# Conv and attention kernel on one core: engines issue in the order of the text, chains end where their buffers are taken anew, positions are loaded two chunks ahead, three chunks are projected early

## The chip, the cores and the metric

The kernel runs on one core of one Trainium2 chip. The metric is the device time of one execution in microseconds (us). The kernel before takes 2003.53 us (median of 3 runs, 2001.35 to 2005.6).

Five engines matter: TensorE (PE in the profile; PEld is its weight load), VectorE (DVE), ScalarE (ACT), GpSimd (POOL) and SyncE (SP), which only issues transfers here. In the built program each engine has its own list of instructions, and an instruction that needs the result of another engine waits for it.

## The reference

Eight images of 128 channels and 48 x 48 = 2304 positions. Cut to what matters:

```python
# layer 0: group norm, projections with position channels, causal attention
xg = group_norm(x)                                   # 32 groups
x0 = concat([xg, pe])                                # 32 position channels
q, k, v = (leaky_relu(W @ x0 + b) for W, b in ...)   # 128 x 2304 each
x = x + softmax(causal(q.T @ k / sqrt(128))) @ v
# layer 1, on tokens
t = tokens(x)
y = layer_norm(t);  t = t + softmax(y @ y.T) @ y     # full attention
y = layer_norm(t);  t = t + recurrence(batch_norm(y @ W.T))   # a scan over 8 batches
```

Everything is float32.

## The kernel before

A batch has six chunks (`NQ`) of 384 columns (`QC`), three blocks of 128 (`QB`) each. A batch is a causal attention followed by a full attention; the eight batches follow one another, and the recurrence closes the kernel. In the full attention some exponentials are stored to DRAM turned (`e`) and loaded back (`g`), so that they are not computed twice. The attention loop is software pipelined: scores of item n are issued, then the product of item n - lag, then `st.tick` may issue one step of the side work (projections, norms, tails of finished chunks), which waits in *chains*:

```python
class Stream:
    def run(self, chain):
        work, cost, delay = chain.steps.popleft()
        work()
        self.now += cost
        chain.at = self.now + delay
        ...
    def tick(self, cost):
        self.now += cost
        for chain in self.chains:
            if chain.at <= self.now:
                self.run(chain)
                return
```

`now` is a clock of the text: it counts the estimated TensorE time of what has been written so far. A step comes into the text when this clock says that its inputs should be there. In the kernel before, the text is only a proposal: a scheduler in the build orders the instructions of each engine anew.

The parts of the causal attention that the argument touches:

```python
def begin(j, m, first):
    if first:
        st.finish(projected[b, j])
        if j + 2 < NQ:
            projected[b, j + 2] = st.add(project(b, j + 2))
    s = psum_s(...);  matmul(s, keys, queries[b, j])
    p = pp.tile(...);  nc.scalar.activation(p, s, Exp)
    if m >= QB * j:                                   # three diagonal blocks come first
        nc.gpsimd.tensor_mul(p[:, off:off+P], ..., triu)      # the mask, on GpSimd
    ...  nc.vector.tensor_add(acc, acc, p)            # row sums

def causal(j, o):                                     # after the last product of chunk j
    def residual():
        tp = psum_t(...);  matmul(tp, ones, acc)      # dn
        nc.vector.reciprocal(r, tp)
        nc.vector.tensor_mul(r, o, r)
        nc.gpsimd.tensor_add(t1, xt, r)               # the residual, on GpSimd too
    ...                                               # tokens (tt), normed (xhT), back (tb)
    st.add([(residual, 0.7, 5.5), (tokens, 0.5, 4.5), (normed, 0.0, 2.0), (back, 0.5, 0.0)])

attention(listed(chunks), 2, begin, product, causal)  # lag 2
```

In `project`, `normed` loads the positions `pb` of a chunk where they are used, then `xn` and three products `pj` follow, each with `z = pj + pb`, a leaky ReLU and a maximum on VectorE. In the full attention, `full` has a chain of six steps for each finished chunk: sums, residual (`ot`), keep (`tk`), normed (`x`), back (`tx`, `xc`), statistics (`wx`). Chunks 0 and 1 of the next batch are projected during the full attention.

## Time and profile before

| | kernel before |
|---|---|
| time, median of 3 | 2003.53 us |
| span of the profiled run | 2000.6 us, mean granted clock 0.978 |
| PE / DVE / ACT / POOL busy | 94 / 64 / 37 / 13% |
| one batch (from the chain of waits) | 227.0 us |

TensorE is the bound, so what counts is the time that it stands idle, or runs at half clock afterwards (four products of 384 columns from 715.79 us start 0.63 us apart instead of 0.32, and the granted clock from 713 to 721 us is 0.79). The prediction shows the lines for this. Two more views are needed later. First the waits of TensorE, largest first; the columns are what waited, for what, us in total, how often, and the longest:

```profile
PE o_causal L913 <- DVE r L926: 21.6, 9, 3.9
PE tx L846 <- DVE x L841: 19.1, 9, 2.2
```

The wait for a mask is far down the list: 0.9 us, once. Second, the timeline of GpSimd at the start of a causal chunk (start, busy us, what, and in brackets the idle time before it and its releaser):

```profile
571.20 0.45 POOL L897 TENSOR_TENSOR p<-p,triu 128x128 f32<-128x128 f32 x1 [7.29 <-ACT p L895]
572.17 0.46 POOL L897 TENSOR_TENSOR p<-p,triu 128x128 f32<-128x128 f32 x1 [0.52 <-ACT p L895]
573.57 0.46 POOL L897 TENSOR_TENSOR p<-p,triu 128x128 f32<-128x128 f32 x1 [0.95 <-ACT p L895]
576.30 1.18 POOL L928 TENSOR_TENSOR t<-x,r 128x384 f32<-128x384 f32 x1 [2.27 <-DVE r L926]
```

The scheduler has put the three masks of the new chunk first (so it is in every chunk of the built program), each running as soon as its exponential is done, and the residual of the finished chunk (`t<-x,r`), which waits for VectorE, behind them.

### The profile page before, as it was taken

The numbers are of one execution on the slowest core, as the hardware profiler recorded it, in microseconds if no ns is written. First come the engines' busy times: TensorE is split into PE (matmuls) and PEld (weight loads), VectorE is DVE, ScalarE is ACT, GpSimd is POOL, SyncE is SP. The second block draws the span as 40 slices with busy tenths as digits, with TensorE's granted clock in tenths as the row PEclk, the third lists the DMA queues.
The fourth block names the chain that finished last, engine by engine and source line by source line (L and its number), as shares of the span: only waits on it lengthen the run. The fifth ranks groups of instructions, "written<-read, shape, count | busy, mean of one in ns | idle before, by whom it ended". The sixth has DMA issues, their size and how long they took to land.

```text
span 2000.6 us, 22146 instructions
## 1 busy us (share of the span) xinstructions
PE 1884.1 (94%) x6760; PEld 1153.8 (58%) x6760; DVE 1280.1 (64%) x3174; ACT 740.6 (37%) x1940; POOL 258.0 (13%) x359
## 2 busy tenths in 40 slices
PE   7899989999999989999999999999999999999793
PEld 4556656665566656665566655665566655665462
DVE  5577558764877558764777559765677549663263
ACT  2244323442245313442245423442245413442352
POOL 1110012001110112001110112101110112101000
PEclk9999999999999999999999999999999999999897
DMA  2105530354105530344205531344205530244504
GB/s 85 42 29 183 150 95 24 107 177 113 66 12 193 154 103 24 107 160 116 80 12 182 159 98 36 107 150 115 91 12 170 160 97 25 68 152 137 212 1 191
DMA packets 106061, 209.85 MB, mean 105 GB/s; under 512 B 12041, under 2 KB 80268, under 8 KB 103886
## 3 DMA queue, kind: packets, MB, share of 16 engines
q1 hardware_dynamic: 104832, 207.66, 32.6%
q8 instruction: 56, 0.92, 0.2%
q10 hardware_dynamic: 1102, 0.68, 0.1%
q14 instruction: 71, 0.58, 0.1%
HBM read 115.11 MB, written 93.19 MB: 104 GB/s over the span
## 4 chain that ended last, share of the span: by engine, by line
PE 85%; DVE 8%; issue 3%; ACT 2%; POOL 1%; DMA 0%; SPq 0%; ACTq 0%; POOLq 0%; DVEq 0%
PE o_full L1030 16%; PE s L1015 16%; PE o_causal L913 14%; PE s L893 12%; PE o_full L1026 11%; PE pj L801 2%; PE z L1185 2%; PE wx L1090 2%; PE z L1163 2%; PE dn L923 1%; PE pj L804 1%; DVE t L1066 1%; PE tx L846 1%; DVE acc L908 1%; DVE z L806 1%
## 5 line engine op out<-in xcount | busy, mean ns | idle before, releaser
L1017 ACT ACTIVATE p<-s,shift 128x384 f32<-128x384 f32 x504 | 293.0, 581 | 465.7 <-PE s L1015 459.0
L895 ACT ACTIVATE p<-s 128x384 f32<-128x384 f32 (+2 forms) x504 | 228.9, 461 | 511.1 <-PE s L893 288.7
L1030 PE MATMUL o_full<-p,xhT 128*128 128x384 f32 x1008 | 409.4, 490 | 0.0
L1015 PE MATMUL s<-xh 128*128 128x384 f32 x1008 | 404.1, 488 | 0.0
L913 PE MATMUL o_causal<-p,vT 128*128 128x384 f32 (+2 forms) x1008 | 362.0, 467 | 23.4 <-DVE r L926 21.6
L893 PE MATMUL s<-q,k 128*128 128x384 f32 (+2 forms) x1008 | 369.1, 459 | 8.1 <-DVE k L811 3.8
L1026 PE MATMUL o_full<-g,xhT 128*128 128x384 f32 x720 | 283.1, 500 | 0.5 <-DMA g<-e 0.5
L908 DVE TENSOR_TENSOR acc<-acc,p 128x384 f32<-128x384 f32 (+1 forms) x408 | 221.5, 543 | 79.8 <-ACT p L895 73.6
L913 PEld LDWEIGHTS o_causal<-p,vT 128*128 128x128 f32 x1008 | 188.3, 195 | 139.9 <-issue 40.6
L985 DVE STREAM_TRANSPOSE t<-p 128x384 f32<-128x384 f32 x360 | 197.4, 563 | 105.5 <-ACT p L1017 104.4
L1030 PEld LDWEIGHTS o_full<-p,xhT 128*128 128x128 f32 x1008 | 189.7, 191 | 125.0 <-issue 3.2
L1015 PEld LDWEIGHTS s<-xh 128*128 128x128 f32 x1008 | 183.4, 191 | 104.4
L893 PEld LDWEIGHTS s<-q,k 128*128 128x128 f32 x1008 | 174.0, 190 | 102.1 <-ACT p L895 8.9
L1026 PEld LDWEIGHTS o_full<-g,xhT 128*128 128x128 f32 x720 | 139.1, 196 | 95.1 <-issue 10.7
L806 DVE TENSOR_TENSOR z<-pj,pb 128x384 f32<-128x384 f32 x144 | 79.1, 549 | 133.6 <-DMA pb<-posb_d 103.4
L994 DVE TENSOR_REDUCE tsum<-t 128x12 f32<-128x1152 f32 x120 | 161.4, 1345 | 2.1
L925 DVE RECIPROCAL r<-dn 128x384 f32<-128x384 f32 x48 | 122.5, 2551 | 12.0 <-PE dn L923 12.0
L897 POOL TENSOR_TENSOR p<-p,triu 128x128 f32<-128x128 f32 x144 | 68.6, 479 | 420.3 <-ACT p L895 420.0
L618 POOL TENSOR_TENSOR rs_f<-ve_l,mhalf 128x3 f32<-128x3 f32 x48 | 43.6, 907 | 588.1 <-DVE ve_l L617 588.1
L1017 ACT ACTIVATION_READ_ACCUMULATOR p<-s,shift 128x1 f32 x504 | 97.2, 193 | 0.0
L928 POOL TENSOR_TENSOR t<-x,r 128x384 f32<-128x384 f32 x48 | 55.3, 1152 | 261.4 <-DVE r L926 244.9
L1066 DVE SCALAR_TENSOR_TENSOR t<-ot,ri,t1t 128x128 f32<-128x128 f32 x144 | 41.6, 340 | 68.3 <-PE ot L846 68.3
(188 smaller groups left out, 1656.4 us busy)
## 6 DMA issues: line engine op xcount, KB each, us to landing
e<-t SPq DMA_DIRECT2D x120, 576.0 KB, 3.2
g<-e SPq DMA_DIRECT2D x480, 144.0 KB, 3.1
pb<-posb_d SPq DMA_DIRECT2D x42, 576.0 KB, 3.7
x<-in_x_dram SPq DMA_DIRECT2D x16, 576.0 KB, 5.1
t_d<-t2c SPq DMA_DIRECT2D x48, 192.0 KB, 1.9
t2o<-t_d SPq DMA_DIRECT2D x8, 1152.0 KB, 9.6
out_dram<-t2o SPq DMA_DIRECT2D x8, 1152.0 KB, 6.6
posb_d<-pb SPq DMA_DIRECT2D x6, 576.0 KB, 2.8
```

Source lines behind the costliest of these rows:

```text
L806: nc.vector.tensor_add(z, ps[:, :QC], c["pb"][:, j, :])
L893: nc.tensor.matmul(s[:, off:QC], keys[b][:, ts(m, P)], queries[b, j][:, off:], start=True, stop=True)
L895: nc.scalar.activation(p[:, off:], s[:, off:QC], AF.Exp, scale=SCALE)
L908: nc.vector.tensor_add(a[:, off:], a[:, off:], p[:, off:])
L913: nc.tensor.matmul(o[:, off:QC], vals[b][:, ts(m, P)], p[:, off:], start=first, stop=last)
L925: nc.vector.reciprocal(r, tp[:, :QC])
L985: nc.vector.transpose(t[:, :, :, g, :].rearrange("p b j r -> p j b r"), p.rearrange("p (j b r) -> p j b r", j=QB, b=R))
L994: nc.vector.tensor_reduce(tsum[j][:, n - j - 1, :], t.rearrange("p b j m r -> p (b j) (m r)"), AX.X, ALU.add)
L1015: nc.tensor.matmul(s[:, :QC], xh[:, ts(m, P)], xh[:, ts(j, QC)], start=True, stop=True)
L1017: nc.scalar.activation(p, s[:, :QC], AF.Exp, bias=shift, accum_out=rows[:, m, j : j + 1])
L1026: nc.tensor.matmul(out_ap, xhT[:, QB * i + g, :], p, start=first, stop=last)
L1030: nc.tensor.matmul(o[:, :QC], xhT[:, what[1], :], p, start=first, stop=last)
```

## The change

The intent: take the ordering away from the scheduler and let every engine issue in the order of the text, which the stream's clock has arranged; with it, end a chain of steps only when a buffer that it uses is taken anew, load positions two chunks before they are used, and project three chunks of the next batch early (one of the `qp` buffers more, one of `small` less). Cut to its core:

```diff
     def add(self, steps, after=0.0):
-        chain = Chain(steps, self.now + after)
+        before, after = after if isinstance(after, tuple) else (None, after)
+        chain = Chain(steps, self.now + after, before)     # may follow another chain
@@
-        qp = actx.enter_context(tc.tile_pool(name="qp", bufs=3))
+        qp = actx.enter_context(tc.tile_pool(name="qp", bufs=4))
@@
+        def owned(tag, owner):
+            before = owners.setdefault(tag, deque([None, None]))
+            chain = (before.popleft() or {}).get("chain")
+            before.append(owner)
+            if chain is not None:
+                st.finish(chain)                           # end the chain that holds the buffer
@@
+        order.enter_context(tc.manual_schedule())          # every engine: order of the text
+        EARLY = 3
@@
+        def load_positions(b, n):
+            if 0 < b < B:
+                pos[b, n] = pbp.tile([P, 3, QC], F32, tag="pb", name=f"pb_{b}_{n}")
+                nc.sync.dma_start(pos[b, n], posb_d[:, n])
@@ def normed():
-                    c["pb"] = pbp.tile(...);  nc.sync.dma_start(c["pb"], posb_d[:, n])
+                    c["pb"] = pos.pop((b, n))
@@ def part(2):
+                        load_positions(*divmod(b * NQ + n + 2, NQ))
@@ def causal(j, o, holder):
-                normed_chunks[j] = st.add([(residual, 0.7, 5.5), (tokens, ...), (normed, ...), (back, ...)])
+                first = st.add([(residual, 0.7, 0.0)])
+                holder["chain"] = whose[j]["chain"] = first
+                c["chain"] = normed_chunks[j] = st.add([(tokens, 0.5, 4.5), (normed, 0.0, 2.0), (back, 0.5, 0.0)], (first, 5.5))
@@ full attention, begin
-                    if j == NQ - 1:
+                    if j == NQ - 2:
                         st.finish(normed_x["chain"])
-                        both = st.add(project(b + 1, 0) + project(b + 1, 1))
+                        steps = [s for n in range(EARLY) for s in project(b + 1, n)]
+                        early = st.add(steps)
@@ ... chunk tiles get an owner, full's chain too; three chunks of batch 0 ...
```

More of the change, by code (lines that the diff above doesn't have):

```diff
@@ L533, with __init__ @@
 class Chain:
-    def __init__(self, steps, at):
-        self.steps, self.at = deque(steps), at
+    def __init__(self, steps, at, before=None):
+        self.steps, self.at, self.before = deque(steps), at, before
 class Stream:
@@ L546, in add @@
     def add(self, steps, after=0.0):
-        chain = Chain(steps, self.now + after)
+        before, after = after if isinstance(after, tuple) else (None, after)
+        chain = Chain(steps, self.now + after, before)
+        if before is not None:
+            before.follower = chain, after
         self.chains.append(chain)
@@ L551, in run @@
     def run(self, chain):
+        if chain.before is not None:
+            self.finish(chain.before)
+        if not chain.steps:
+            return
         work, cost, delay = chain.steps.popleft()
-        work()
+        if not chain.steps:
+            self.chains.remove(chain)
         self.now += cost
         chain.at = self.now + delay
-        if not chain.steps:
-            self.chains.remove(chain)
+        work()
+        if not chain.steps and hasattr(chain, "follower"):
+            follower, after = chain.follower
+            follower.before, follower.at = None, self.now + after
     def tick(self, cost):
@@ L561, in tick @@
         for chain in self.chains:
-            if chain.at <= self.now:
+            if chain.before is None and chain.at <= self.now:
                 self.run(chain)
@@ L566, in finish @@
     def finish(self, chain):
+        if chain.before is not None:
+            self.finish(chain.before)
         while chain.steps:
@@ L627, in fast_path @@
         gpool = actx.enter_context(tc.tile_pool(name="gpool", bufs=3))
-        qp = actx.enter_context(tc.tile_pool(name="qp", bufs=3))
+        qp = actx.enter_context(tc.tile_pool(name="qp", bufs=4))
         work = actx.enter_context(tc.tile_pool(name="work", bufs=2))
-        small = actx.enter_context(tc.tile_pool(name="small", bufs=4))
+        small = actx.enter_context(tc.tile_pool(name="small", bufs=3))
         ps_s = actx.enter_context(tc.tile_pool(name="ps_s", bufs=4, space=PSUM))
@@ L639, in psum_t, with psum_o, chunk_tile @@
             return ps_t.tile([P, CH], F32, tag="t", name=name)
-        def psum_o(name):
+        owners = {}
+        def owned(tag, owner):
[4 more added lines that the diff above has]
+                st.finish(chain)
+        def psum_o(name, owner):
+            owned("o", owner)
             return ps_o.tile([P, CH], F32, tag="o", name=name)
-        def chunk_tile(tag, name):
+        def chunk_tile(tag, name, owner=None):
+            if owner is not None:
+                owned(tag, owner)
             return work.tile([P, QC], F32, tag=tag, name=name)
@@ L721, in fast_path @@
         st = Stream()
+        order = ExitStack()
+        order.enter_context(tc.manual_schedule())
+        EARLY = 3
         norm_of = {}
@@ L760, in fast_path @@
         keys, vals, queries, largest, projected = {}, {}, {}, {}, {}
+        pos = {}
+        def load_positions(b, n):
+            if 0 < b < B:
+                pos[b, n] = pbp.tile([P, 3, QC], F32, tag="pb", name=f"pb_{b}_{n}")
+                nc.sync.dma_start(pos[b, n], posb_d[:, n])
         def project(b, n):
@@ L785, in normed @@
                 if b:
-                    c["pb"] = pbp.tile([P, 3, QC], F32, tag="pb", name=f"pb_{b}_{n}")
-                    nc.sync.dma_start(c["pb"], posb_d[:, n])
+                    c["pb"] = pos.pop((b, n))
                 if n == 0:
@@ L815, in f @@
                         )
+                    else:
+                        load_positions(*divmod(b * NQ + n + 2, NQ))
                 return f
@@ L861, in attention @@
                     if first:
-                        o[j] = psum_o(f"o_{after.__name__}_{n}")
-                    cost += product(j, what, o[j], ready.pop(n - lag), first, last)
+                        owner = {}
+                        o[j] = psum_o(f"o_{after.__name__}_{n}", owner), owner
+                    cost += product(j, what, o[j][0], ready.pop(n - lag), first, last)
                     if last:
-                        after(j, o.pop(j))
+                        after(j, *o.pop(j))
                 st.tick(cost)
@@ L878, in causal_attention @@
             normed_chunks = {}
-            sums = {}
+            sums, whose = {}, {}
             def offset(j, m):
@@ L886, in begin @@
                     st.finish(projected[b, j])
-                    if j + 2 < NQ:
-                        projected[b, j + 2] = st.add(project(b, j + 2))
+                    if j + EARLY < NQ:
+                        projected[b, j + EARLY] = st.add(project(b, j + EARLY))
                     if j == NQ - 1:
@@ L900, in begin @@
                 elif sums[j][1] is None:
-                    a = chunk_tile("acc", f"acc_{b}_{j}")
+                    whose[j] = {}
+                    a = chunk_tile("acc", f"acc_{b}_{j}", whose[j])
                     if off:
@@ L914, in product, with causal @@
                 return (QC - off) * US
-            def causal(j, o):
+            def causal(j, o, holder):
                 cols = ts(j, QC)
@@ L923, in residual @@
                     nc.tensor.matmul(tp[:, :QC], ones, acc, start=True, stop=True)
-                    r = chunk_tile("r", f"r_{b}_{j}")
+                    r = chunk_tile("r", f"r_{b}_{j}", c)
                     nc.vector.reciprocal(r, tp[:, :QC])
                     nc.vector.tensor_mul(r, o[:, :QC], r)
-                    c["t1"] = chunk_tile("t1", f"t1_{b}_{j}")
+                    c["t1"] = chunk_tile("t1", f"t1_{b}_{j}", c)
                     nc.gpsimd.tensor_add(c["t1"], xt[:, cols], r)
@@ L945, in back @@
                     nc.scalar.copy(xh[:, cols], tp[:, :QC])
-                normed_chunks[j] = st.add([(residual, 0.7, 5.5), (tokens, 0.5, 4.5), (normed, 0.0, 2.0), (back, 0.5, 0.0)])
+                first = st.add([(residual, 0.7, 0.0)])
+                holder["chain"] = whose[j]["chain"] = first
+                c["chain"] = normed_chunks[j] = st.add([(tokens, 0.5, 4.5), (normed, 0.0, 2.0), (back, 0.5, 0.0)], (first, 5.5))
             chunks = [list(range(QB * j, QB * (j + 1))) + list(range(QB * j)) for j in range(NQ)]
@@ L1002, in begin @@
                         normed_x["chain"] = st.add(group_norm(b + 1))
-                    if j == NQ - 1:
+                    if j == NQ - 2:
                         st.finish(normed_x["chain"])
-                        both = st.add(project(b + 1, 0) + project(b + 1, 1))
-                        projected[b + 1, 0] = projected[b + 1, 1] = both
+                        steps = [s for n in range(EARLY) for s in project(b + 1, n)]
+                        early = st.add(steps)
+                        for n in range(EARLY):
+                            projected[b + 1, n] = early
                 prefetch()
@@ L1031, in product, with full @@
                 return QC * US
-            def full(j, o):
+            def full(j, o, _):
                 cols = ts(j, QC)
                 c = {}
-                o_sb = chunk_tile("acc", f"o_sb_{b}_{j}")
+                o_sb = chunk_tile("acc", f"o_sb_{b}_{j}", c)
                 nc.scalar.copy(o_sb, o[:, :QC])
@@ L1063, in residual @@
                     tp = transposed(o_sb, f"ot_{b}_{j}")
-                    t2 = chunk_tile("r", f"t2_{b}_{j}")
+                    t2 = chunk_tile("r", f"t2_{b}_{j}", c)
                     for g in range(QB):
@@ L1073, in keep @@
                     tp = transposed(c["t2"], f"tk_{b}_{j}")
-                    t2c = chunk_tile("t2c", f"t2c_{b}_{j}")
+                    t2c = chunk_tile("t2c", f"t2c_{b}_{j}", c)
                     nc.scalar.copy(t2c, tp[:, :QC])
@@ L1078, in normed @@
                 def normed():
-                    c["x2"] = chunk_tile("t1", f"x2_{b}_{j}")
+                    c["x2"] = chunk_tile("t1", f"x2_{b}_{j}", c)
                     normalize(c["x2"], c["t2"], c["mv"], c["rs"])
@@ L1083, in back @@
                     tp = transposed(c["x2"], f"tx_{b}_{j}")
-                    c["xc"] = chunk_tile("xc", f"xc_{b}_{j}")
+                    c["xc"] = chunk_tile("xc", f"xc_{b}_{j}", c)
                     nc.scalar.copy(c["xc"], tp[:, :QC])
@@ L1091, in statistics @@
                     nc.vector.bn_stats(stats[:, b * NQ + j, :], tp[:, :QC])
-                st.add([
+                c["chain"] = st.add([
                     (sums, 0.1, 1.5), (residual, 0.4, 2.0), (keep, 0.4, 1.5), (normed, 0.0, 2.0),
@@ L1110, in fast_path @@
         st.finish(st.add(group_norm(0)))
-        for n in range(2):
+        for n in range(EARLY):
             projected[0, n] = st.add(project(0, n))
@@ L1117, in fast_path @@
             st.run(st.chains[0])
+        order.close()
     SEGS = 32
```

## The prediction

> **What bounds the kernel now.** I read the page first: busy time by engine, then the forty slices.
>
> ```profile
> PE 1884.1 (94%) x6760; PEld 1153.8 (58%) x6760; DVE 1280.1 (64%) x3174; ACT 740.6 (37%) x1940; POOL 258.0 (13%) x359
> PE   7899989999999989999999999999999999999793
> DVE  5577558764877558764777559765677549663263
> ```
>
> TensorE (PE) is busy 94% of the span, VectorE (DVE) 64%. The DVE row has a period of about four and a half slices: eight batches, each with a dense causal attention (7 and 8) and a thinner full attention. The last four slices are the recurrence, which the change leaves alone. In the chain of waits in order of time the same 2.33 us "issue" gap returns at 294.22, 520.43, 748.33, 974.47, 1202.37, 1428.47 and 1656.39 us, so a batch takes (1656.39 - 294.22) / 6 = 227.0 us.
>
> How much of that is needed? The PE timeline inside the causal phase shows the dense pace:
>
> ```profile
> 563.32 0.81 PE L913 MATMUL o_causal<-p,vT 128*128 128x384 f32 x2
> 563.97 0.81 PE L893 MATMUL s<-q,k 128*128 128x384 f32 x2
> 564.61 0.81 PE L913 MATMUL o_causal<-p,vT 128*128 128x384 f32 x2
> 565.25 0.49 PE L846 MATMUL tb<-ident,xhT 128*128 128x128 f32 x3
> 565.58 0.81 PE L893 MATMUL s<-q,k 128*128 128x384 f32 x2
> ```
>
> Starts are 0.645 us apart for 384 columns and 0.33 us for three transposes (the ends, 0.81, are modelled). Counted from the code, a batch has 43,776 columns of causal products, 65,664 of full attention, 6,912 of projections, 4,608 of `dn` and `wx`: 120,960 / 384 x 0.645 = 203.2 us. Thirty groups of three transposes add 9.8 us, and small sums, group norm and short-matmul overhead about 1.8. Need: 214.8 us. **Lost: 12.2 us per batch, seven times, at the change of batch**, which the PE timeline there shows:
>
> ```profile
> 710.61 0.84 PE L846 MATMUL tk<-ident,t 128*128 128x128 f32 x3 [0.22 <-DVE t L1066]
> 713.57 0.84 PE L846 MATMUL tx<-ident,x 128*128 128x128 f32 x3 [2.12 <-DVE x L841]
> 715.04 0.91 PE L1090 MATMUL wx<-xc,w1T 128*128 128x384 f32 x2 [0.62 <-ACT xc L1085]
> 715.79 2.70 PE L1026 MATMUL o_full<-g,xhT 128*128 128x384 f32 x4
> 718.29 1.29 PE L1030 MATMUL o_full<-p,xhT 128*128 128x384 f32 x2
> ...
> 730.34 0.91 PE L893 MATMUL s<-q,k 128*128 128x384 f32 x2 [0.43 <-ACT p L895]
> 733.75 0.55 PE L846 MATMUL ot<-ident,o_sb 128*128 128x128 f32 x3 [0.57 <-ACT o_sb L1037]
> 739.57 0.91 PE L893 MATMUL s<-q,k 128*128 128x384 f32 x2 [0.39 <-DVE k L811]
> 751.49 0.88 PE L913 MATMUL o_causal<-p,vT 128*128 128x384 f32 x2 [2.17 <-DVE r L926]
> ```
>
> The tail of chunk 4 (ot, tk, tx, wx) stands in one block and PE waits out its latencies: 0.22 + 2.12 + 0.62, about 4.1 us with restarts. Then o_full runs at 1.28 us per 384 columns until 719.4 (+1.9). Then 0.43, 0.57 and 0.39, about 2.0 with restarts, and 2.17 for `r`, followed in every other batch by another slow stretch (x14 in 5.80 us at 523.59). Together 11.4 or 13.1 us.
>
> Behind the last waits stands DVE's own hole:
>
> ```profile
> 716.60 0.42 DVE L904 TENSOR_TENSOR acc<-p,p 128x256 f32<-128x256 f32 x1
> 731.40 0.56 DVE L806 TENSOR_TENSOR z<-pj,pb 128x384 f32<-128x384 f32 x1 [14.38 <-DMA pb<-posb_d]
> ```
>
> The position load for chunk 2 stands in the SP queue behind 20 `g<-e` issues (694.32 to 725.96) and a store, so it is issued at 726.4. DVE stands 14.4 us, then runs nearly full from 731 to 760, and `k` and `r` come late.
>
> [...]
>
> **The change part by part.** I compared the built instruction orders engine by engine.
> 1. *Nothing of weight is removed or added*: the same matmuls, vector operations and bytes. Only order and buffers differ (`qp` 3 to 4, `small` 4 to 3). The need stays 214.8 us.
> 2. *Positions early.* Chunks 0 and 1 of the next batch are loaded in the causal phase; `pb` of chunk 2 now stands in the SP order ahead of the last six `g` groups of the batch, and over 7 us of DVE work lie before its first reader, against 3.7 us from issue to landing (page, part 6). The 14.4 us hole goes.
> 3. *Three chunks projected early.* Chunk 2's DVE work (xn, three z, three leaky, two maxima: 9 x 0.47 = 4.2 us) moves from the crowded start of the causal phase into full attention, where DVE is idle half the time. In the new order `dn` of chunk 0 precedes the first use of its bank by o_causal by 5.8 us of PE work; reciprocal and product need 2.5 + 0.5. The 2.17 wait goes, as do those for `k` and ACT `p`: 2.3 + 0.3 (a smaller `r` wait at 538.9) + 2.0 us with restarts, and every other time 2.5 us of slow clock: about 6 per batch.
> 4. *Text order.* The tail of chunk 4 is now spread: 2.6 us of PE work between ot and tk, 4.5 between tk and tx. Its 4.1 + 1.9 us go.
> 5. *Chains end when buffers are taken anew.* This puts back a stall: chunk 5's tail is forced by the second `acc` tile of the next batch, so tk, tx, wx stand in a row in the PE order. From the end of ot: t2 0.9, moments 1.0, POOL root 1.0 or `z,q,largest` 1.5 in its shadow, normalise 0.8, so tx is done some 4.5 us after ot; PE has 2.5 us of work there. That is 2.0 of waiting if DVE comes at once; three `acc` operations stand ahead of t2 in DVE's order, so I take 2.6. Then the ACT copy, 0.65. Also the first o_causal waits for exp 0.49 and mask 0.48 behind only 0.65 us of matmuls: 0.65. [...]and about 0.4 of restarts. New loss 6.0 per batch.
>
> Sum per change of batch: 12.2 - 6.0 = 6.2; times seven, **44 us**. Last batch: the block of chunk 4 at 1836 to 1846 (0.57 + 0.45 + 2.12 + 0.62 and slow clock) goes: 4.5 us. Batch 0 gets worse: it cannot project early, begins chunks 1 and 2 with a wait for `k` (1.3 each), and `dn` of chunks 0, 1, 2 stands only 0.9 to 1.5 us ahead of the product that needs the bank (about 2 each), 9 us with 3 of clock against 1.24 + 3.92 and 3.4 of clock now: -3.5, with 1 us back in the prologue. Sum 44 + 4.5 - 2.5 = 46: **2003.5 - 46 = 1957.5 us**.
>
> **Rivals.**
> - *In-order waiting eats the gain.* Program order on all engines at once lets one late operation stop everything behind it. For: DVE runs at 95% while projections last (31 us of PE work against some 30 of DVE in chunks 0 to 2); POOL's 1.16 us residual waits for `r` ahead of the masks. Against: I found only 1 to 2 us of DVE lag, and 4 score banks and 6 `p` tiles cover that. If each batch loses 4 us more: 1985.
> - [...]
> - *Only the transfer mattered.* If the tail block returns whole with chunk 5 (4.1 + 1.9), the gain is 6 per batch, 1962: nearly the same.
> - *The load was hidden anyway.* Speaks against: PE waits for `k` and `r` only after the hole. It would leave 1990.
>
> **Range and chances.** Floor for everything that sits at the batch change is 12.2 x 7 = 85, so 1918; the first rival gives 1985. I take 1935 to 1982. The 2% line is 1963.5, close to my number: faster 0.60, same 0.37, slower 0.03.
>
> **What would show it right or wrong.** Right: no `z` wait on the `pb` transfer; batch period near 221 us; no 2.17 wait of o_causal for `r` after batch 0; one remaining cluster per batch at tx and wx, on chunk 5. Wrong: new PE waits spread through the causal phase (for POOL masks, `p` or `acc`), or DVE waits for `g` or `e` buffers in full attention[...].

## The result and the profile after

| | before | after |
|---|---|---|
| time, median (range), 4 runs each | 2004.09 us (2001.35 to 2005.6) | 2062.08 us (2060.15 to 2071.48) |
| ratio, 95% interval | | 1.030 (1.0267 to 1.0334) |
| one batch | 227.0 us | 235.7 us |
| TensorE wait for a mask (`o_causal <- POOL p`) | 0.9 us, once | 33.9 us, 28 times |
| half-clock stretches, 30 to 1830 us | 11, 31.3 us | 17, 48.3 us |

A ratio is the mean time of one kernel's runs over that of the other's runs of the same rounds, so it is not quite the ratio of the medians. The half-clock stretches are counted from the TensorE timeline: matmuls of 384 columns that start 0.64 us apart instead of 0.32, without idle time between them. The batch period after is from the chain of waits, where the same 3.56 us "issue" piece returns at 335.92, 571.55, 807.17, 1042.79, 1278.38 and 1514.20: (1514.20 - 335.92) / 5 = 235.7.

The page's first and second part:

```profile
PE 1896.0 (92%) x6760; PEld 1158.6 (56%) x6760; DVE 1345.6 (65%) x3174; ACT 745.6 (36%) x1940; POOL 262.3 (13%) x359
PE   6899999999899998999889998999989999999893
DVE  5667666665857667666758568676667658574253
```

The counted instructions are the same in number on every engine. TensorE falls from 94 to 92% of a longer span. VectorE's curve has lost some of its period, as intended: the projections are spread. The waits of TensorE:

```profile
PE o_causal L950 <- POOL p L933: 33.9, 28, 2.2
PE tb L881 <- DVE xhT L876: 23.4, 16, 2.0
PE pj L834 <- DVE xn L827: 16.9, 15, 1.6
PE tx L881 <- DVE x L876: 15.6, 8, 2.5
```

The 103.4 us for which VectorE waited for `pb` (7 times) are gone, and so is the 2.17 us wait of `o_causal` for `r` at the batch change. In their place stand three waits that the kernel before hardly had (`p`, `tb`, `pj`), spread through the causal phase, and the one that the prediction foresaw at the tail of chunk 5:

```profile
521.36 0.84 PE L881 MATMUL tx<-ident,x 128*128 128x128 f32 x3 [1.88 <-DVE x L876]
522.82 0.91 PE L1131 MATMUL wx<-xc,w1T 128*128 128x384 f32 x2 [0.62 <-ACT xc L1126]
```

Now the mask. The timeline of GpSimd in the same kind of place as before:

```profile
570.12 0.46 POOL L933 TENSOR_TENSOR p<-p,triu 128x128 f32<-128x128 f32 x1 [2.67 <-ACT p L931]
571.09 0.46 POOL L933 TENSOR_TENSOR p<-p,triu 128x128 f32<-128x128 f32 x1 [0.52 <-ACT p L931]
575.14 0.99 POOL L965 TENSOR_TENSOR t<-x,r 128x384 f32<-128x384 f32 x1 [3.60 <-DVE r L963]
576.10 0.46 POOL L933 TENSOR_TENSOR p<-p,triu 128x128 f32<-128x128 f32 x1
```

The residual now stands *between* the second and the third mask. The reason is in the text: the last product of chunk j - 1 comes, with a lag of two, between items 1 and 2 of chunk j, and `residual` is written at the first tick that has nothing older to do; items 0, 1 and 2 are the three diagonal blocks. In the built order the residual stands ahead of the third mask in chunks 4 and 5 of every batch from the second on, and in chunks 2, 3 and 4 of the first; in the other chunks projections take the tick, and the residual comes behind the mask or ahead of the next chunk. On GpSimd the third mask, ready some 3.7 us earlier (its exponential ended at 572.35), waits until the residual has had its operand. Its operand comes late, and the chain of waits of the next chunk shows why (start, us, what):

```profile
592.87 0.47 POOL p L933
...
593.36 0.43 DVE acc L941
593.79 2.48 DVE r L962
...
596.29 0.57 DVE r L963
...
597.00 0.99 POOL t L965
597.99 0.42 POOL p L933
...
598.45 0.49 PE o_causal L950 x2
...
599.59 1.09 PE o_causal L950 x2
600.67 1.28 PE s L929 x2
```

Of the 28 waits, four fall in each batch from the second on; at this place they are 0.52 us (515.75, a mask of chunk 0), 0.25 (554.75, chunk 3, where a root of a normalisation stands ahead of the third mask), 1.87 (576.60, chunk 4) and 2.20 (598.45, chunk 5). The two behind a residual make 7 x (1.87 + 2.20) = 28.5 of the 33.9 us. In the first batch no wait for a mask is listed, although the residual stands ahead there too.

In the chain above: a mask, an add on VectorE, a reciprocal of 2.48 us, a multiply, the add on GpSimd, the next mask: 5.6 us in a row (592.87 to 598.45), on which TensorE has about 3.4 us of work. It waits 2.20 us at 598.45, and from 599.59 it runs at half clock (1.09 and 1.28 instead of 0.65; the granted clock from 596 to 604 us is 0.79).

VectorE has its own version of the same thing. Its timeline ahead of a `tb` that TensorE waits 1.77 us for:

```profile
554.93 2.55 DVE L962 RECIPROCAL r<-dn 128x384 f32<-128x384 f32 x1
557.52 0.56 DVE L963 TENSOR_TENSOR r<-o_causal,r 128x384 f32<-128x384 f32 x1
557.99 2.48 DVE L945 TENSOR_TENSOR acc<-acc,p 128x384 f32<-128x384 f32 x3
560.39 0.85 DVE L876 TENSOR_SCALAR xhT<-t1t,mv_c,rs_c 128x128 f32<-128x128 f32 x3
```

The normalisation `xhT` (line L876) stands behind a reciprocal, a multiply and three adds, without a gap between them: VectorE isn't idle, it does other things first. The last input of `xhT`, a root on GpSimd (0.85 us at 553.41), was there at 554.3; it starts at 560.39, 6 us later. The text clock had left 2.0 us between `xhT` and `tb`.

### The profile page after: what moved, and what is told of

Its sections match the earlier page's. It is cut to its first block, busy times and chain, and to the rows that moved or that the text cites. A ratio compares the mean times of both kernels' runs of the same rounds, so it can differ in the third digit from the quotient of the medians. Undisturbed runs are those within 1.5% of the kernel's fastest.

```text
span 2059.9 us, 22117 instructions
## 1 busy us (share of the span) xinstructions
PE 1896.0 (92%) x6760; PEld 1158.6 (56%) x6760; DVE 1345.6 (65%) x3174; ACT 745.6 (36%) x1940; POOL 262.3 (13%) x359
## 4 chain that ended last, share of the span: by engine, by line
PE 70%; DVE 20%; issue 4%; POOL 2%; ACT 2%; DMA 1%; POOLq 0%; SPq 0%; DVEq 0%; ACTq 0%
PE s L1056 14%; PE o_full L1071 13%; PE o_full L1067 10%; PE o_causal L950 10%; PE s L929 10%; DVE r L962 4%; DVE acc L945 3%; DVE z L839 2%; PE z L1227 2%; PE wx L1131 2%; PE pj L834 2%; DVE largest L846 2%; PE z L1205 2%; DVE q L844 1%; DVE gn_st L760 1%
## 5 line engine op out<-in xcount | busy, mean ns | idle before, releaser
L950 PE MATMUL o_causal<-p,vT 128*128 128x384 f32 (+2 forms) x1008 | 392.1, 474 | 40.2 <-POOL p L933 33.9
L929 PE MATMUL s<-q,k 128*128 128x384 f32 (+2 forms) x1008 | 389.3, 471 | 3.8 <-DVE k L844 3.8
L1067 PE MATMUL o_full<-g,xhT 128*128 128x384 f32 x720 | 278.9, 488 | 0.0
L929 PEld LDWEIGHTS s<-q,k 128*128 128x128 f32 x1008 | 186.6, 197 | 99.2 <-issue 16.4
L1067 PEld LDWEIGHTS o_full<-g,xhT 128*128 128x128 f32 x720 | 132.8, 190 | 81.9 <-issue 0.4
L834 PE MATMUL pj<-xn,wT 128*128 128x384 f32 x192 | 81.6, 511 | 16.9 <-DVE xn L827 16.9
```

Of the source, the lines that this page charges most:

```text
L834: nc.tensor.matmul(ps[:, :QC], wT[:, j, :], xn, start=True, stop=True)
L929: nc.tensor.matmul(s[:, off:QC], keys[b][:, ts(m, P)], queries[b, j][:, off:], start=True, stop=True)
L950: nc.tensor.matmul(o[:, off:QC], vals[b][:, ts(m, P)], p[:, off:], start=first, stop=last)
L1067: nc.tensor.matmul(out_ap, xhT[:, QB * i + g, :], p, start=first, stop=last)
```

## The experiments

The theory after reading the two traces: the text order on GpSimd and VectorE costs more than everything else gains. Rivals: the ending of chains (the chunk 5 tail), or the order on TensorE itself. The first kernels take parts away from the kernel after, the later ones try the other parts without the text order. Two came out clearly outside every range that I had written down: e8 was 10 us and g2 27 us faster. h2, b4 and b6, of which my theory said 1940 to 1970, came out as the rival said, h2 3 us beyond it. The others lie in one of their ranges or within 3 us of its edge.

Seventeen kernels ran, 3 rounds each, 4 runs of each kernel. All outputs are right. The kernel before, run alongside, had medians of 2002.3, 2002.9, 2003.5, 2002.4 and 2002.5 us, so medians may be compared within a microsecond or two.

| run | what differs | median us | ratio to before (95%) |
|---|---|---|---|
| (after) | | 2062.1 | 1.030 (1.0267 to 1.0334) |
| e1_no_text_order | scheduler orders all engines | 1972.1 | 0.986 (0.983 to 0.988) |
| e2_text_order_alone | text order, no early positions or third chunk | 2101.9 | 1.048 (1.046 to 1.051) |
| e3_pool_free | POOL by the scheduler | 2002.1 | 1.001 (0.999 to 1.003) |
| e5_dve_free | DVE by the scheduler | 2020.2 | 1.009 (1.008 to 1.011) |
| e7_pe_act_sp_text | POOL and DVE by the scheduler | 1975.7 | 0.987 (0.984 to 0.990) |
| k3_pool_alone_text | only POOL in text order | 2006.0 | 1.002 (1.000 to 1.004) |
| e4_residual_later | residual 1.5 us later in the text | 2018.2 | 1.008 (1.007 to 1.010) |
| e8_split_tail | second `acc` tile ends only two steps | 2028.5 | 1.013 (1.011 to 1.014) |
| b4_mended_text | e4, e8 and more slack, all in text order | 2004.6 | 1.001 (0.999 to 1.003) |
| b6_mended_free | b4, POOL and DVE by the scheduler | 1978.3 | 0.988 (0.986 to 0.990) |
| h2_pe_text_split | e7 with e8 | 1982.9 | 0.990 (0.987 to 0.992) |
| k1_ending_chains_alone | no text order; only chains end at buffers | 1984.2 | 0.991 (0.990 to 0.993) |
| g1_positions_alone | k1 and positions early | 1968.5 | 0.982 (0.981 to 0.984) |
| g2_early_chunks_alone | k1 and three early chunks | 1943.4 | 0.969 (0.968 to 0.971) |
| l1_positions_one_ahead | e1, positions one chunk ahead | 1954.5 | 0.976 (0.974 to 0.978) |
| k2_early_chunks_split | g2 with e8 | 1945.9 | 0.972 (0.970 to 0.973) |
| l2_early_chunks_residual_later | g2 with e4 | 1943.8 | 0.970 (0.969 to 0.972) |

### Is it the text order?

e1_no_text_order takes it away and keeps the rest:

```diff
-        order.enter_context(tc.manual_schedule())
+        pass
```

> The change with the text order taken away (the scheduler orders again); early positions, three early chunks and ending chains kept. Theory A (in-order waiting costs the 58 us and eats a gain that early positions and projections do bring): 1965 to 1995, batch period about 222 to 226 us, no long wait of z for pb. Rival B (positions and early projections are worth nothing or cost time themselves): 2004 or more. Rival C (the early projections crowd DVE whatever the order): about 2060.

Measured: 1972.1 us. The text order costs 2062.1 - 1972.1 = 90 us, and without it the change is a gain of 1.4%, clear of noise but under the 2% line. e2_text_order_alone does the opposite: text order and ended chains, but positions loaded where they are used and two early chunks as before.

```diff
-        EARLY = 3
+        EARLY = 2
@@ full attention, begin
-                    if j == NQ - 2:
+                    if j == NQ - 1:
@@ normed
-                    c["pb"] = pos.pop((b, n))
+                    c["pb"] = pbp.tile(...);  nc.sync.dma_start(c["pb"], posb_d[:, n])
```

> Text order and ending chains alone: two chunks early, positions loaded where they are used. Theory A (in-order waiting costs): slower than the change, 2075 to 2100, the z wait for pb back and the POOL mask waits kept. Rival C (three early chunks are the cost): faster than the change, 2010 to 2040.

Measured: 2101.9 us, 118 us more than the same kernel without the text order (k1 below, 1984.2). So the other parts of the change soften what the text order costs; they don't cause it.

### Which engine's order?

The text order can be asked for by engine. e3_pool_free leaves GpSimd to the scheduler, e5_dve_free VectorE, e7_pe_act_sp_text both:

```diff
-        order.enter_context(tc.manual_schedule())
+        order.enter_context(tc.manual_schedule(engines={PE, DVE, Activation, SP}))    # e3
+        order.enter_context(tc.manual_schedule(engines={PE, Pool, Activation, SP}))   # e5
+        order.enter_context(tc.manual_schedule(engines={PE, Activation, SP}))         # e7
```

> The change with text order on PE, DVE, ACT and SP but not on POOL: the built PE and DVE orders are the same row for row, on POOL the third diagonal mask of a chunk stands ahead of the residual add and of the root instead of behind. Theory A1 (PE waits 34 us for masks that stand behind a POOL operation waiting for DVE[...]): 2005 to 2020, PE waits for POOL p under 8 us. Rival A2 (DVE's order is the cost, tb, tx and pj waits of 56 us): 2045 to 2060, the waits only move.

> The change with text order on every engine but DVE; PE and POOL orders the same row for row. Theory A1 (POOL's order is the cost): 2045 to 2060, mask waits kept at 25 us or more. Rival A2 (DVE's order: tb waits for xhT 23 us, pj for xn 17, tx for x 16): 2000 to 2020, tb and pj waits under 10 us in sum.

> Text order on PE, ACT and SP, free order on DVE and POOL. If POOL's order (60 us in e3) and DVE's order (42 us in e5) are costs that add: about 1960. If they share waits, so that either freed engine already takes part of the other's: 1970 to 1990. If PE's own text order costs time: over 1972, the run with no text order at all.

e3 is the sharpest of all, because no other engine's order moves. A comparison of the built programs (rows of each engine's order, e3 against the kernel after):

```
## PE: 7314 rows in the other, 7314 in this; the same
## DVE: 7243 rows in the other, 7243 in this; the same
## ACT: 3213 rows in the other, 3213 in this; the same
 L933 TensorTensor p_2_7_400<-p_2_7_400,triu 128x128
+L933 TensorTensor p_2_8_419<-p_2_8_419,triu 128x128
 L965 TensorTensor t_0_0_408<-x_121,r_0_405 128x384
-L933 TensorTensor p_2_8_419<-p_2_8_419,triu 128x128
```

The edit lets the third mask (`p_2_8`) pass the residual, and so on in each place where the residual stood ahead of one; a few masks also pass the root of a normalisation (chunks 1 and 3), where 0.25 us a batch was waited for. Measured: 2002.1 us, so POOL's order alone is worth 60 us. TensorE's wait for masks in e3's profile:

```profile
PE o_causal L950 <- POOL p L933: 3.6, 7, 0.5
```

It falls from 33.9 to 3.6. The 60 us add up as follows: 30.3 from this wait, 23.4 - 16.9 = 6.5 from `tb`, and half clock: 15.8 us in 6 stretches against 48.3 in 17, half of the difference is 16 (the mean granted clock is 0.985 against 0.977). That is 53, less 1.6 by which `pj` waits longer; I take the remaining 8 or 9 to be restarts after the waits (in the kernel after, three transposes held TensorE for 0.58 us after the wait that ended at 560.88, and for 0.33 us without one at 516.50), an estimate that no run separates.

e5: 2020.2 us, so VectorE's order is worth 42 us. Here `tb` falls from 23.4 to 3.6 and `pj`'s wait for `xn` vanishes from the list of the larger ones, while the wait for masks stays:

```profile
PE o_causal L950 <- POOL p L933: 32.1, 21, 2.2
PE tb L881 <- DVE xhT L876: 3.6, 14, 0.3
```

e7: both free, 1975.7 us, within 4 us of e1, where TensorE, ScalarE and SyncE were free too. **Measured against e1, the order of the text on TensorE, ScalarE and SyncE cost 4 us; the order on GpSimd and VectorE cost 86 us.** The 4 us are a net: in e7 `tx` waits 20.5 us where it waits 11.8 in e1, `tb` 4.0 where it waits 8.9. And e1 is not the best order that the scheduler found (g2 below); on that kernel a fixed order of TensorE was not tried. The orders of GpSimd and VectorE are not independent. Starting from e7, VectorE's order alone costs 26 us (e3), GpSimd's 44 (e5), both 86. A likely reason is that the masks wait for VectorE's reciprocal and VectorE's adds wait for the masks, so that a fixed order on one makes the other's dearer; no run isolates it.

k3_pool_alone_text (`engines={Pool}`) fixes the order of GpSimd alone:

> Text order on POOL alone, everything else of the change free, against 1972 us with no text order at all. If POOL's fixed order is a cost by itself (the third mask behind the residual add): 1995 to 2030, PE waits for POOL p of 15 us or more. If it only costs because PE's order is fixed too and nothing else can be put in its place: within 8 us of 1972.

Measured: 2006.0 us, 34 us above e1:

```profile
PE o_causal L950 <- POOL p L933: 34.9, 36, 1.6
```

No half-clock stretch is left between 30 and 1830 us (mean granted clock 0.988), so here the waits, with their restarts, make the loss without it. A kernel that leaves everything else to the scheduler loses its gain to this one order.

### One place in the text

If the mechanism is right, the residual's place is what matters. e4_residual_later puts it 1.5 us later in the text, so past the third mask, in all-text order:

```diff
-                first = st.add([(residual, 0.7, 0.0)])
+                first = st.add([(residual, 0.7, 0.0)], 1.5)
```

> The change, all engines in text order, with one number different: the residual step of a causal chunk falls due 1.5 us later, so that in chunks 4 and 5 the third diagonal mask is issued ahead of the residual's dn, reciprocal and POOL add. Theory A1 (the mask stands behind the POOL add that waits for DVE's reciprocal, 2.0 and 2.4 us[...]): 2005 to 2025, PE waits for POOL p under 12 us. Rival (the mask would wait anyway, for ACT or a crowded POOL): 2050 to 2062.

Measured: 2018.2 us. One number takes back 44 us. In the built program the residual now stands behind all three masks in every chunk. The edit moves its `dn`, reciprocal and multiply on TensorE and VectorE too, so it is less pure than e3. The wait for masks falls by 28.5 us, just what the two places behind a residual had cost, while VectorE's waits stay, as this line shows for `tb`:

```profile
PE o_causal L950 <- POOL p L933: 5.4, 14, 0.5
PE tb L881 <- DVE xhT L876: 23.0, 15, 2.0
```

### The tail of chunk 5

The chain of a full-attention chunk ends when the second `acc` tile of the next batch is taken, although only its first two steps read that tile. e8_split_tail lets the tile own those two steps alone:

```diff
-                o_sb = chunk_tile("acc", f"o_sb_{b}_{j}", c)
+                opened = {}
+                o_sb = chunk_tile("acc", f"o_sb_{b}_{j}", opened)
@@
-                c["chain"] = st.add([(sums, ..), (residual, ..), (keep, ..), (normed, ..), (back, ..), (statistics, ..)])
+                opened["chain"] = first = st.add([(sums, 0.1, 1.5), (residual, 0.4, 0.0)])
+                c["chain"] = st.add([(keep, ..), (normed, ..), (back, ..), (statistics, ..)], (first, 2.0))
```

> The change with the o_sb tile owned by the first two steps of its tail alone, so that taking the acc buffer anew no longer forces tk, tx and wx of chunk 5 in a row. The predicted stall there (x 1.9, xc 0.6 and restarts, about 3.0 us at seven changes of batch) should go: 2038 to 2045, PE waits for x at tx from 15.6 to under 4 us. Rival (the tail then waits elsewhere, or collides with DVE's crowded opening of the causal phase): 2055 or more.

Measured: 2028.5 us, 34 us less. The foreseen stall at `tx` goes:

```profile
PE o_causal L950 <- DVE acc L940: 42.8, 17, 2.8
PE tx L881 <- DVE x L876: 2.5, 1, 2.5
PE tb L881 <- DVE xhT L876: 1.9, 2, 1.6
```

`tx` falls from 15.6 to 2.5 us. But the first line was 6.3 us in the kernel after: new waits stand at two products early in the causal phase (2.47 us at 529.50, 2.77 at 549.43), and in sum they are larger than what `tx` gave back. The gain comes from elsewhere too. The edit shifts the text behind it, and with that the order of every engine: `tb` falls from 23.4 to 1.9 us, and the wait for masks from 33.9 to 25.6, because the residual now stands behind the third mask in chunk 4. So the 34 us are not the worth of the foreseen stall; no run isolates that. And the gain exists in text order only. With GpSimd and VectorE free, the same edit gives 1982.9 instead of 1975.7 (h2_pe_text_split), and on the best kernel 1945.9 instead of 1943.4 (k2_early_chunks_split).

> Text order on PE, ACT and SP, DVE and POOL free, and the split tail: the run of 1976 us with its tx waits (20.5 us[...]) taken away. Theory (each cost is removed by what made it): 1940 to 1960. Rival (the tx waits only move to the banks that the tail holds): 1968 to 1980.

> The fastest version so far (1943 us: free order, three early chunks, positions loaded where used) with the split tail. If the order in which tail steps are written still weighs when the scheduler is free: 1930 to 1940. If not: within 4 us of 1943.

### Can the text be mended?

b4_mended_text keeps every engine in text order and repairs what the traces showed: the tail split, the residual 1.5 us later, `back` 4 instead of 2 us after its normalisation, `xn` 3 instead of 1 us ahead of its products, projections at the lowest priority in `tick`. b6_mended_free is the same text with GpSimd and VectorE left to the scheduler.

```diff
+   residual 1.5 us later and split tail, as in e4 and e8
-   (normed, 0.0, 2.0), (back, 0.5, 0.0)          # causal
+   (normed, 0.0, 4.0), (back, 0.5, 0.0)
-   [(normed, 0.0, 1.0)]                          # project
+   [(normed, 0.0, 3.0)]
-   for chain in self.chains:
+   for chain in sorted(self.chains, key=lambda c: getattr(c, "low", False)):   # project: low
```

> All engines in text order, with the text mended: residual 1.5 us later, split tail, transposes back due 4 instead of 2 us after their normalisation, first projection 3 instead of 1 us after xn, projections last among the chains that are due. Theory A (text order is not slow as such, it was slow where a step was issued before its inputs were ready): 1945 to 1970, mask, tb, pj and tx waits of PE under 25 us in sum. Rival (any fixed order on DVE and POOL costs): 2000 or more.

> The mended text (residual later, split tail, slack, projections last) with text order on PE, ACT and SP alone. Theory (the mended text left DVE's fixed order as the only cost, tb waits of 33 us): 1940 to 1960, tb waits under 10 us. Rival (with DVE and POOL free the mending is worth nothing beyond the split tail): equal to the run beside it within 5 us.

Measured: 2004.6 and 1978.3 us. The repairs take the text-ordered kernel back to the time of before and not below it; I had expected 1945 to 1970. The largest wait in b4:

```profile
PE tb L881 <- DVE xhT L876: 33.5, 14, 4.3
```

The wait for masks is 13.2 us in b4. Freeing the two engines brings another 26 us, but not from `tb`, which waits as long in b6:

```profile
PE tb L881 <- DVE xhT L876: 33.4, 7, 4.8
```

Only TensorE, ScalarE and SyncE are in text order there, so VectorE's text order is not what keeps it: TensorE stands at `tb` for 4.78 us at 511.47 while VectorE does a reciprocal (2.53 us at 506.79) before the small operation (509.23) that leads to `xhT`. Whether TensorE's fixed order is the cost here, no run isolates. And b6 is within 5 us of h2, which has the split tail alone, and 3 us slower than e7, which has neither: with GpSimd and VectorE free, the mending was worth nothing.

### What the other parts give

Without the text order, k1_ending_chains_alone has only the ended chains (with `qp` 4 and `small` 3), g1_positions_alone adds the early positions, g2_early_chunks_alone adds the third early chunk instead. Their edits are those of e1 and e2 in other combinations.

> The kernel before with the ending of chains alone (and qp 4, small 3), free order, two chunks early, positions loaded where used. If the ending of chains is bookkeeping that only text order needs: 1998 to 2006. If it makes the scheduler take residuals earlier, as the 11 us shorter first batch of all free runs suggests: 1980 to 1992.

> The kernel before with positions loaded two chunks ahead (and the bookkeeping of ending chains), two chunks early as before, no text order. Of the 30 us that the change without text order gains: if the late transfer (14.4 us of standing DVE per batch) was the whole cause, 1970 to 1980; if DVE's load at the start of the causal phase matters beside it, 1985 to 1998.

> The same with three chunks projected early and the positions loaded where they are used, no text order. If the projected chunk is what matters, 1970 to 1985; if the transfer is what matters, its wait returns in full attention and the time is 1990 to 2010.

Measured: 1984.2, 1968.5 and **1943.4 us**. The ended chains (with the changed buffer numbers, which no run separates) bring 18 us, early positions another 16, the third early chunk, instead of those, another 41. k1 already does much of what the prediction expected of the other parts: TensorE's wait for `r` (21.6 us before) is gone from its list, and VectorE's for `pb`, 103.4 us before, is down to 24.8 (7 times, longest 4.5) although the positions are loaded where they are used. From k1 to g2 TensorE's waits at the tails of the full attention fall: `tx` for `x` from 20.5 to 4.4 us, `wx` from 5.6 to 1.2, `ot` from 5.1 to 1.1; and the half-clock stretches between 30 and 1830 us fall from eight to one (mean granted clock 0.981 and 0.988). In g2 the largest waits of TensorE outside the prologue and the recurrence are small, those 4.4 us for `tx` and, for `tb`:

```profile
PE tb L880 <- DVE xhT L875: 4.3, 15, 0.4
```

A batch takes about 220.0 us, 5.2 above the 214.8 that the prediction worked out as the need.

Both together (e1) should have been better still and are worse, 1972.1 us. VectorE's largest wait in e1 tells where the hole went:

```profile
DVE z L839 <- PE pj L834: 122.2, 18, 12.8
```

The 103.4 us for `pb` of the kernel before have become 122.2 us for `pj`: with its positions loaded, `z` is put into VectorE's order earlier than TensorE's `pj` is into its own, and VectorE stands up to 12.8 us in front of it. To see whether the lead is the cause, l1_positions_one_ahead loads them one chunk ahead instead of two:

```diff
-                        load_positions(*divmod(b * NQ + n + 2, NQ))
+                        load_positions(*divmod(b * NQ + n + 1, NQ))
```

> Text order off, three chunks projected early, positions loaded early, but each only one chunk ahead instead of two (1972.1 us with two, 1943.4 us with each loaded where it is used). Theory: with positions ready long before, the scheduler, which goes by when it thinks an operand is ready, puts the next chunk's vector work ahead of the acc adds of the chunk at hand, and the order it then finds is worse; with a shorter lead less of that: between 1945 and 1962, and DVE's z waits for PE pj, 122 us with two ahead, under 80. Rival: any preloading at all disturbs (two pb buffers held, loads in another place of the SP order): 1968 to 1976, waits as with two ahead.

Measured: 1954.5 us, and the wait of `z` for `pj` is 40.7 us (8 times), with 29.4 us for `pb` (3 times) beside it. The lead is a cause: a shorter one gives back 18 of the 29 us. How the scheduler weighs the operands was not looked into, and why, with three early chunks, any preloading is still 11 us worse than none stays open. The last run checks that the residual's place in the text matters only where the text is binding (g2 with the edit of e4):

> The best kernel so far (three early chunks, scheduler's order, positions where used, 1943.4 us) with the residual 1.5 us later in the text. Theory: where GpSimd and VectorE are ordered by the scheduler the place in the text is only a hint, so the edit that took 44 us off the text-ordered kernel takes nothing here: within 6 us of 1943. Rival: the residual is placed too early in every order: 5 to 20 us less, 1925 to 1938.

Measured: 1943.8 us, no difference.

**The best version is g2_early_chunks_alone**: chains ended at their buffers, three early chunks, positions loaded where they are used, order by the scheduler. It is 3.1% faster than the kernel before and takes 1943.4 / 2062.1, 5.8% less, than the kernel after.

## Why the prediction was wrong

I expected 1957.5 us, faster with a chance of 0.60, and gave slower 0.03. It became 2062.1, outside the range by 80.

- *Where the bound lies and what a batch needs*: right. The need of 214.8 us a batch is what g2 comes close to (5.2 above it). One sum on the way does not come out: the losses listed at the change of batch, 4.1 + 1.9 + 2.0 + 2.17, make 10.2 and not 11.4; the 12.2 that the forecast uses is 227.0 - 214.8 and does not rest on them.
- *Part 2, positions early*: half right. The wait on the `pb` transfer disappeared. Its worth was put into part 3 and the sum; measured alone it is 16 us. But early positions were not needed to close most of VectorE's hole (103.4 us for `pb` before, 24.8 in k1), and with the scheduler they open another (e1, 122.2 us for `pj`).
- *Part 3, three early chunks*: right in size by luck. I put about 6 us a batch, for the waits for `r`, `k` and `p`; 1984.2 - 1943.4 = 41 us over seven changes of batch is 5.8. But the wait for `r` is already gone in k1; what the third chunk takes away there is mostly the waits of the tails and half clock, which I had booked to part 4.
- *Part 5, ended chains*: right for the place, the cluster at `tx` and `wx`, and too high in size: I wrote 2.6 and 0.65, and the trace has 1.88 and 0.62, with 0.52 for the first mask where I wrote 0.65. That is 3.0 us of waits a batch against 3.9, and the loss at half clock that I also counted in the 6.0 did not come at that place. (Elsewhere such a stretch has that size: in the kernel before the granted clock from 484 to 494 us is 0.83, by estimate 10 x 0.17 = 1.7 us lost.) e8 took 34 us off by removing the stall, but not from there alone. With the scheduler, ended chains are no loss; they gain 18 us (k1).
- *Part 4, "Text order", is the step that failed.* I counted for it only a gain, the spread tail of chunk 4 (4.1 + 1.9 us a batch), and nothing for what a fixed order on VectorE and GpSimd costs. Measured, text order costs 90 us, some 12 a batch (235.7 against 223.7 in e1), and 86 of it go when these two engines are freed (e7): GpSimd's order alone is worth 60 us (e3), where TensorE waited 33.9 us for masks, VectorE's 42 (e5), where it waited 23.4 us at `tb` and 16.9 at `pj`.
- *The rival that came true was on the page.* I named it ("In-order waiting eats the gain", with "POOL's 1.16 us residual waits for `r` ahead of the masks") and set it aside with "I found only 1 to 2 us of DVE lag, and 4 score banks and 6 `p` tiles cover that". Two errors are in that sentence. Spare buffers let TensorE run ahead with scores, but in the trace matmuls stay in order: the product of item 2 waits for its mask until 598.45, and the scores behind it start at 598.78, after it. In the text, TensorE has only two further items of slack (lag 2), here 3.4 us of work; 5.6 us of serial work on VectorE and GpSimd don't fit into it. And I walked through the order at the batch change and the first chunks, where projections push the residual elsewhere; it stands ahead of the third mask in chunks 4 and 5. A look at those chunks of the built order would have shown it, because it is visible without a chip.
- *The signs for wrong* came true in part: waits in the causal phase for masks. TensorE also ran at half clock in about two stretches a batch (17 in all). The period was 235.7 us and not 221. The signs for right came true as well (no `z` wait on the `pb` transfer, no 2.17 wait for `r`, one cluster on chunk 5): they watched the seam, and the loss was elsewhere.

The size of what failed is clear, but the division among masks, `tb` and half clock within the 60 and 42 us is estimated from the waits, not isolated.

## What to carry to other kernels

A fixed order is only as good as the time estimates behind it, and these were estimates of TensorE's time alone: check each helper engine whose order is fixed for an instruction with a late operand standing in front of one that the bound engine needs soon, and do so in the steady state, not just at the seam that you want to mend. Fix the order engine by engine: here TensorE, ScalarE and SyncE together could be fixed for 4 us beside e1, while GpSimd's order alone undid the gain. Test the parts of a bundle alone and in pairs: the best version has two of the four parts, and a third made it worse. And when a forecast part comes out in size, look whether its waits are the ones that went.

## What the traces show of the engines

- TensorE's half pace came after single gaps in the kernel after: 1.77 us (`tb` at 560.88, half pace from 562.11) and 2.20 us (598.45, half pace from 599.59); one of 1.87 us (576.60) was not followed by it, so here the length alone does not decide, and these gaps give no border. In k3 no gap between 30 and 1830 us was followed by it (mean granted clock 0.988), with waits for masks of up to 1.6 us. In the kernel after, the half-pace stretches together lasted 48.3 us, so by estimate half of that, 24 us, were lost.
- GpSimd kept to the built order in the kernel after: a mask whose exponential had ended at 572.35 started at 576.10, after the residual ahead of it. What such an order costs a kernel whose helper engines work for producers of different urgency: here 60 us for GpSimd (e3), 42 us for VectorE (e5).
- A reciprocal of 128 x 384 float32 on VectorE takes 2.55 us, an add of the same shape 0.55 (kernel after). The reciprocal is the largest term of the chain that delays the mask.
